# Counting keys for a top-64 search: one of VectorE's eight blocks handed to ScalarE

## The chip, the cores and the metric

The kernel runs on one core of a Trainium2 chip. The metric is device time in microseconds (us) of one execution. Three runs of the kernel before took 2841.61, 2842.69 and 2843.36 us, so the median is 2842.69 us.

The engines are called by their names in the profile: PE is TensorE (matrix products), PEld its weight loads, ACT is ScalarE, DVE is VectorE, POOL is GpSimd and SP is SyncE. Each works through its own instruction list in order and waits for others by semaphores.

## The reference, cut to what matters

Two transformer layers on eight sequences of 512 tokens. The part that the change touches is the attention of the first layer: 16 heads, 64 memory keys ahead of the sequence's own keys, a causal mask, and of each row's scores only the 64 largest kept.

```python
dots = jnp.einsum('bhid,bhjd->bhij', q, k) * SCALE
dots = jnp.einsum('bhij,hk->bkij', dots, pre_proj)
...
kth = jax.lax.top_k(dots, TOPK)[0][..., -1:]
dots = jnp.where(dots < kth, mask_value, dots)
attn = jax.nn.softmax(dots, axis=-1)
attn = jnp.einsum('bhij,hk->bkij', attn, post_proj)
out = jnp.einsum('bhij,bhjd->bhid', attn, v)
```

Beside it stand a feed-forward part quantised to 4 bits and, after it, a second layer. They aren't touched.

## The kernel before, in words

**Stages.** After some 150 us of preparation the attention of all eight sequences runs as one long planned stage, up to about 2287 us; the rest (the feed-forward part of seven sequences and the second layer) follows behind a branch on a flag and takes 552 us.

**Groups and blocks.** The attention is cut into 64 groups, eight for each sequence, in the order 7, 0, 5, 2, 6, 1, 4, 3 (`ORDER`). A group holds eight blocks. A block is a tile of 128 rows (16 heads by 8 tokens) by all the keys that these tokens can see: 72 keys for the first block of group 0, 8 more for each block on, 576 for the last block of group 7. Four groups are in flight at once, since the ring of score buffers has four places.

**The way of a group.** PE makes the scores and ACT copies them out of PSUM (L1037, L1043). The search (L1181) then looks for a threshold in each row that about 60 scores exceed. `begin` puts a first guess into `cur`. A round counts, block by block, how many scores lie above `cur` (`count`, L1072), and `narrow` (L1088) makes a better threshold from the eight counts. After the last round, `off` says how far the count is from the aim, `under` (L1135) takes the eight scores next to the threshold (two passes of DVE over each block), and `pick` (L1145) takes the one of them that is the 64th. ACT makes the exponentials (L1158), DVE keeps those that pass (L1167) and inverts their sum (L1252), POOL makes the mixing matrices `mixd` (L1260), and PE turns the scores with them (L1283) and multiplies with the values (L1307); ACT copies each product out of PSUM (L1289, L1321).

**The rounds.** Each round is a pair: how many of the eight blocks ACT counts, and whether POOL does `narrow` (else DVE does). In `ROUNDS`, the rule for 58 of the 64 groups, ACT counts all eight blocks of the first three rounds and POOL narrows; DVE counts all eight of the last three and narrows twice, and after the third it makes `off`. `EDGE`, for the first two groups, shares five rounds half and half between ACT and DVE. `LAST`, for the last four groups (60 to 63), has three rounds on ACT, two shared half and half, and a sixth on DVE alone.

**Two kinds of counts.** ACT's count is a Sign with a sum, so a block yields below minus above; DVE's is a comparison times -2, so it yields -2 times the number above. `base` holds, for each number of blocks on ACT, what has to be added to make both the same quantity; `narrow` begins with `base - raw` (L1099). The last round before was DVE's alone, and its `off` (L1209) is made with fixed numbers.

**What sets the order.** A planner written in Python (`Plan`, L81) orders every engine's list before the kernel runs. Each operation has an engine, an estimated cost, the operations that it needs and a due time; whichever is ready first on its engine goes next, the earlier due one where two are close. So a change of one operation's engine moves many others. DMAs of this stage are issued by SP, and none belongs to the search.

## Time and profile before

The profiled execution took 2840.84 us, of which the span from the first to the last instruction is 2839.1 us.

| | busy us | share of the span | instructions |
|---|---|---|---|
| PE | 2539.6 | 89% | 19064 |
| PEld | 1966.9 | 69% | 19064 |
| DVE | 2439.3 | 86% | 7978 |
| ACT | 2026.9 | 71% | 5876 |
| POOL | 1206.7 | 43% | 2215 |

| count of a block | instructions | busy us | mean ns |
|---|---|---|---|
| on ACT (L1079) | 1560 | 864.0 | 560 |
| on DVE (L1083) | 1512 | 828.0 | 580 |

The shares are means over the whole span, over stages with different limits. In the 40 slices of the profile PE is nine tenths busy or more from the second slice to the 30th, while DVE stands between eight and nine tenths and ACT between seven and eight. In the 31st and 32nd slice (about 2129 to 2271 us) PE falls to six tenths and less, and DVE stays at nine. That is why the prediction reads windows of time and not the page's totals alone.

### The profile page before, as it was taken

What the parts mean: (1) busy time and instruction counts of PE and PEld (TensorE: products, weight loads), DVE (VectorE), ACT (ScalarE), POOL (GpSimd) and SP (SyncE); (2) the same over time, 40 slices, a digit from 0 to 9 for tenths busy, and PEclk for the clock granted to TensorE, in tenths of its full rate; (3) what the DMA queues carried; (4) which work ended last, traced back from release to release, by engine and by line L of the source; (5) the groups of instructions that cost most, each with busy time, mean ns of one, the idle gap of its engine ahead of it and who ended that gap; (6) DMA issues with size and microseconds to landing.
All of it is one profiled execution on the core that took longest, in us unless ns stands there. A gap on an engine that the chain in (4) does not pass through costs nothing. (4 is left out here: it accounts for less than half of the span.)

```text
span 2839.1 us, 57481 instructions
## 1 busy us (share of the span) xinstructions
PE 2539.6 (89%) x19064; PEld 1966.9 (69%) x19064; DVE 2439.3 (86%) x7978; ACT 2026.9 (71%) x5876; POOL 1206.7 (43%) x2215
## 2 busy tenths in 40 slices
PE   5999999999999999999999999999986578999997
PEld 3677777777777778777787777778765455666664
DVE  6678989989989998999899889999999969877762
ACT  3478887788788878887888788788897444644442
POOL 3203544345444544444453545455445344444320
PEclk9999999999999999999999999999987788999998
DMA  4300010100000000000000010000110031000000
GB/s 135 148 24 16 27 30 16 29 18 19 21 25 18 28 18 27 20 18 26 21 19 18 25 29 17 16 23 20 35 42 5 8 109 30 23 16 15 8 8 15
DMA packets 114871, 82.70 MB, mean 29 GB/s; under 512 B 79339, under 2 KB 108806, under 8 KB 113798
## 3 DMA queue, kind: packets, MB, share of 16 engines
q1 hardware_dynamic: 114566, 78.95, 9.1%
q8 instruction: 153, 2.51, 0.4%
q14 instruction: 152, 1.25, 0.1%
HBM read 44.04 MB, written 35.39 MB: 28 GB/s over the span
## 5 line engine op out<-in xcount | busy, mean ns | idle before, releaser
L1079 ACT ACTIVATE junk<-ring,cur 128x312 int8<-128x312 f32 (+27 forms) x1560 | 864.0, 560 | 32.9 <-POOL cur L1132 12.0
L1083 DVE SCALAR_TENSOR_TENSOR junk<-ring,cur,two 128x72 int8<-128x72 f32 (+9 forms) x1512 | 828.0, 580 | 19.7 <-POOL cur L1132 17.7
L1037 PE MATMUL ps_sc<-xnT,tk 128*128 128x8 f32 (+38 forms) x2048 | 536.4, 408 | 37.3 <-ACT ring L1043 36.9
L997 PE MATMUL ps_mi<-rows,mg 128*128 128x128 f32 x4096 | 501.9, 277 | 10.5 <-ACT tk L1008 10.5
L997 PEld LDWEIGHTS ps_mi<-rows,mg 128*128 128x128 f32 x4096 | 480.5, 192 | 39.0 <-issue 13.8
L1037 PEld LDWEIGHTS ps_sc<-xnT,tk 128*128 128x128 f32 x2048 | 348.4, 199 | 185.8 <-issue 89.8
L1283 PE MATMUL ps_at<-mixd,ring 128*128 128x128 f32 (+1 forms) x3072 | 410.4, 284 | 63.1 <-POOL mixd L1260 58.5
L1283 PEld LDWEIGHTS ps_at<-mixd,ring 128*128 128x128 f32 (+1 forms) x3072 | 365.1, 185 | 96.0 <-POOL mixd L1260 72.4
L1167 DVE SCALAR_TENSOR_TENSOR ring<-ring,kth,e 128x520 f32<-128x520 f32 (+56 forms) x512 | 276.1, 561 | 86.2 <-ACT e L1158 84.1
L1099 POOL TENSOR_TENSOR cur<-base,raw 128x8 f32<-128x8 f32 x186 | 50.1, 269 | 658.7 <-ACT junk L1079 626.8
L1079 ACT ACTIVATION_READ_ACCUMULATOR junk<-ring,cur 128x1 f32 x1560 | 303.5, 195 | 0.0
L1289 ACT COPY at<-ps_at 128x512 f32<-128x512 f32 (+1 forms) x384 | 221.9, 581 | 101.5 <-PE ps_at L1283 98.3
L1140 DVE SCALAR_TENSOR_TENSOR y<-ring,cur 128x520 f32<-128x520 f32 (+56 forms) x512 | 288.7, 564 | 3.1
L1043 ACT COPY ring<-ps_sc 128x456 f32<-128x456 f32 (+56 forms) x512 | 184.4, 374 | 125.0 <-PE ps_sc L1037 120.4
L1143 DVE MAX8 top<-y 128x8 f32<-128x520 f32 (+56 forms) x512 | 255.3, 499 | 17.6
L1158 ACT ACTIVATE e<-ring 128x520 f32<-128x520 f32 (+56 forms) x512 | 228.2, 472 | 19.6 <-DVE ring L1167 19.4
L1307 PE MATMUL ps_y<-at,v 128*64 128x64 f32 (+1 forms) x6144 | 225.3, 225 | 16.9 <-ACT at L1289 16.8
L1307 PEld LDWEIGHTS ps_y<-at,v 128*64 128x64 f32 (+1 forms) x6144 | 198.7, 138 | 55.7 <-ACT at L1289 31.6
L1122 POOL TENSOR_TENSOR by<-gap,minus 128x8 f32<-128x8 f32 x124 | 220.5, 1779 | 9.7
L1008 ACT COPY tk<-ps_mi 128x256 f32<-128x256 f32 x512 | 168.0, 377 | 59.4 <-PE ps_mi L997 58.7
L1260 POOL TENSOR_TENSOR mixd<-mix,rden 128x512 f32<-128x512 f32 x128 | 153.1, 1212 | 132.8 <-DVE rden L1252 85.2
L235 PE MATMUL ps_gu<-mg,ring 128*128 128x352 f32 x448 | 148.8, 477 | 15.2 <-DVE hid L235 10.3
(316 smaller groups left out, 3934.7 us busy)
## 6 DMA issues: line engine op xcount, KB each, us to landing
msd<-scr SPq DMA_DIRECT2D x32, 512.0 KB
ring<-msd SPq DMA_DIRECT2D x512, 32.0 KB
scr<-in_L_attn_x_dram SPq DMA_DIRECT2D x10, 512.0 KB
mg_d<-mg SPq DMA_DIRECT2D x1, 4096.0 KB
att<-o SPq DMA_DIRECT2D x64, 64.0 KB
ring<-in_L_attn_x_dram SPq DMA_DIRECT2D x8, 512.0 KB
ring<-att SPq DMA_DIRECT2D x8, 512.0 KB
out_dram<-ring SPq DMA_DIRECT2D x8, 512.0 KB
```

The lines of the kernel that those rows point to most:

```text
L997: nc.tensor.matmul(ps[:, j * P : (j + 1) * P], mg[:, e, k + j, e2 * P : (e2 + 1) * P], toks(e), start=(e == 0), stop=(e == DC - 1),)
L1037: nc.tensor.matmul(ps[:, :ntok], q["tk"][side_of(g)][e][:, b].rearrange("p k i -> p (k i)"), o["xnT"][:, e, :ntok], start=(e == 0), stop=( ...
L1079: nc.scalar.activation(junk, src, AF.Sign, bias=thr, scale=-1.0, accum_out=raw[:, b : b + 1])
L1083: nc.vector.scalar_tensor_tensor(junk, src, thr, two.to_broadcast([P, src.shape[-1]]), ALU.is_ge, ALU.mult, accum_out=raw[:, b : b + 1],)
L1122: eng.tensor_tensor(by, gap[:, 1], minus, ALU.pow)
L1140: nc.vector.scalar_tensor_tensor(y, src, cur[:, 0, b : b + 1], src, ALU.is_ge, ALU.subtract, reverse1=True)
L1143: nc.vector.max(out=top[:, b, :], in_=y)
L1158: nc.scalar.activation(e, src, AF.Exp, scale=1.0 / SMALL)
L1167: nc.vector.scalar_tensor_tensor(src, src, kth[:, b : b + 1], e, ALU.is_ge, ALU.mult, accum_out=den[:, b : b + 1])
L1283: nc.tensor.matmul(pt[:n, b * P : (b + 1) * P], s[:, 4 * j + b, col : col + n], w["mix"][j][:, b, :], start=True, stop=True,)
L1289: nc.scalar.copy(ats[c][:n, :, j * 4 * RB : (j + 1) * 4 * RB].rearrange("p k (b i) -> p b k i", i=RB), w.pop(("pt", c, j))[:n].rearrange(" ...
L1307: nc.tensor.matmul(w["py"][j * DH : (j + 1) * DH, q * GR : (q + 1) * GR], vs[c][:n, k * DH : (k + 1) * DH], ats[c][:n, k, :], start=(c == ...
```

## The change

In `ROUNDS`, ACT now counts one block of eight, the first and so the shortest, in each of the three rounds that DVE had alone. In `LAST`, for the last four groups, the sixth round is shared half and half like the two before it. `EDGE` stays. As the last round may now hold counts of both kinds, `off` is made from `base` like the start of `narrow`; it comes out twice as large as before, with the sign kept, so the constants `io8` that it is compared with are doubled. `base` gets a fourth tile, for one block on ACT.

```diff
-ROUNDS = ((GB, True), (GB, True), (GB, True), (0, False), (0, False), (0, False))
+ROUNDS = ((GB, True),) * 3 + ((1, False),) * 3
 
 EDGE = ((GB // 2, False),) * (len(ROUNDS) - 1) + ((0, False),)
-LAST = ((GB, True),) * 3 + ((GB // 2, False),) * 2 + ((0, False),)
+LAST = ((GB, True),) * 3 + ((GB // 2, False),) * 3
...
             for q in range(8):
-                r.gpsimd.memset(io8[:, q : q + 1], 3.5 - q)
+                r.gpsimd.memset(io8[:, q : q + 1], 7.0 - 2 * q)
...
                         w["off"] = st.tile([P, GB], F32, name="foff", bufs=4)
-                        nc.vector.tensor_scalar(w["off"], w["raw"], -0.5, -AIM, ALU.mult, ALU.add)
+                        nc.vector.tensor_tensor(w["off"], base[na][:, g * GB : (g + 1) * GB], w["raw"], ALU.subtract)
```

In the instruction lists of the two kernels DVE's counts go from 1512 to 1322 and ACT's from 1560 to 1750. DVE instructions that take a round's counts (L1099, L1209) and name a wait for ACT go from 12 to 121, and ACT counts that name a wait for DVE from 12 to 124. The planner orders all engines anew.

## The prediction

> **What bounds the kernel now.** The chain of waits comes first and helps little: it only reaches back to 2287 us, where the last stage begins behind a branch, and the change lies before that. So I read the busy time in windows. I cut the attention stage where PE's slices fall: 150 to 2105 us, with full flow, and 2105 to 2266 us, where the last groups run out. Columns: busy of PE, PEld, DVE, ACT, POOL with instruction counts, granted clock, DMA.

> ```profile
> 150.00:2105.00 1955.00, 1829.97 (x15558) 1478.26 (x15556) 1782.69 (x6549) 1609.93 (x5026) 873.86 (x1821) 0.98 0.08 23
> 2105.00:2266.00 161.00, 97.43 (x748) 78.27 (x749) 154.59 (x467) 104.51 (x289) 69.30 (x105) 0.78 0.02 7
> ```

> In the full flow PE is busy 93.6%, DVE 91.2%, ACT 82.3%. In the run-out DVE is busy 96%, PE 61%, ACT 65%: there DVE alone sets the pace. Next I ask what PE waits for in the full flow, from the waits of PE in that window (waiting line, what it waited for, total us, times, longest).

> ```profile
> PE ps_at L1283 <- POOL mixd L1260: 41.9, 33, 3.4
> PE ps_sc L1037 <- ACT ring L1043: 32.6, 18, 4.1
> PE ps_y L1331 <- ACT y L1321: 19.2, 7, 2.8
> PE ps_mi L997 <- ACT tk L1008: 10.5, 7, 1.7
> PE ps_y L1307 <- ACT at L1289: 9.9, 8, 1.9
> PE ps_mi L968 <- ACT scr L974: 4.0, 1, 4.0
> ```

> All of PE's gaps together are some 120 us: 41.9 us because `mixd` is late, which is DVE's lateness passed on (POOL makes `mixd` once DVE has inverted the sums), and 76 us in these five ACT rows because a copy out of PSUM is late. PE's work doesn't change, so 120 us is all that the full flow could ever give, and the change takes load from the first kind of wait and adds it to the engine behind the second.

> Last, the four longest waits of ACT in the same window.

> ```profile
> ACT ring L1043 <- PE ps_sc L1037: 115.9, 158, 1.6
> ACT at L1289 <- PE ps_at L1283: 90.3, 111, 2.6
> ACT tk L1008 <- PE ps_mi L997: 51.8, 54, 1.6
> ACT scr L974 <- PE ps_mi L968: 21.8, 15, 2.4
> ```

> ACT's idle time, 345 us, is mostly waiting for PE: it has room, but it is held in order in front of PE's products.

> The row first: by busy time PE (93.6%) stands ahead of DVE. [...] I side with the row, because PE's list has only 120 us without work.

> **What is moved.** In 58 groups three counts of the first block go from DVE to ACT: 174. In the last four groups four counts each: 16. That is 1512 - 1322 = 190 in all.

> *DVE, saved.* The mean count of the eight sizes that a first block can have (72, 136, ... 520 keys) is 528, 361, 418, 485, 553, 792, 690, 750 ns. Two are swollen by operations on POOL beside them: at 72 and 392 keys, where the next block, 8 keys longer, takes 279 and 625 ns. With these two in their place the mean is 520 ns. Consecutive counts overlap by 70 ns (in the timeline one of 544 keys lasts 0.77 us and the next instruction starts after 0.69), so 0.45 us is freed each: 174 x 0.45 = 78 us, 87 us with the swollen means.

> *ACT, added.* 371, 411, 459, 507, 569, 628, 678, 741 ns, mean 545; in the timeline the next instruction follows 10 ns earlier, with the reading of the sum inside: 174 x 0.535 = 93 us.

> Both engines then stand at 87% in the full flow (1782.69 - 78 and 1609.93 + 93 over 1955). The trade is poor for small groups (72 keys: 371 ns on ACT for 279 on DVE) and even for large ones. [...]

> *Waits, added.* Each of the 174 counts waits for DVE's `cur`, and DVE's next step (L1099, or L1209 in the last round) waits for ACT's count. The trace has this in the first two and last four groups: 18 steps at L1099 with shared rounds, with DVE idle 3.9 us in 3 of them. So 0.22 us on average, 1.3 us where it happens. From below zero (15 of 18); from above 1.3 us each, 226 us. I take 0.22 for DVE, nearest in kind: 38 us. Behind a waiting L1099 or L1209 stand the passes of `under` and the keeping passes L1167, for which POOL's `mixd` and then PE wait. L1209 is placed straight after the counts, long before `pick` needs it, so its wait is avoidable but paid. Behind a waiting ACT count stand the copies out of PSUM, for which PE waits. The nearest row is ACT before its counts for POOL's `cur`: 11.5 + 10.6 + 4.0 us over some 175 rounds, 0.15 us each, 26 us for 174, and hidden unless PE needs the copy.

> *Small edits.* `off` stays one instruction of 8 numbers (L1209 170 ns, L1099 166 ns): nothing. `base` gets one tile more, 9 settings of 0.1 to 0.15 us on POOL, 1 us in the preparation, where POOL is busy 41 of 120 us; were it not covered, 1 us. No DMA is added, and no queue of SP or POOL is passed.

> **The sum, against the profiled execution (span 2839.1, time 2840.84 us).**

> - Full flow: DVE is relieved of 78 - 38 = 40 us net. PE sees that only through `mixd`'s 41.9 us. Bounds: nothing, and all of it. I take half, -21 us. ACT's work grows by 93/1610 = 6%, and 26 us of holds come on top, another 1.6%; PE's waits for it, 76 us, grow by 0 at best, and at worst by the whole 93. I take 15%, twice the growth in load, as a queue near full grows faster than its load: +12 us. Together -9 us.
> - Run-out: 16 counts at 0.36 to 0.71 us, less the overlap, are 7.4 us, and the last groups of the other kind finish there too, about 2 us. ACT has a third of its time free, so I take four new waits of 0.22 off: -8 us.

> 2840.84 - 17 = 2823.8 us; the median of the runs is 1.85 us above the profiled execution, so 2826 us. The ends: all of `mixd`'s wait and nothing from ACT give 2793 us; nothing from `mixd` and all 93 us on PE give 2928, which would need that ACT never counts while it waits for PE, though it waits 345 us: I don't reach so far. Three quarters of `mixd` with 5% give 2808, a quarter with 20% 2840; the new order of all lists, which no row prices, I put within these.

> **Rivals.**

> *PE holds the full flow, and the run-out gives only half.* For it: 93.6% busy. Against it: `mixd` is late 33 times. -4 us: 2839, within 0.2%.

> *DVE sets the pace.* For it: beside 91% busy it waits 108 us, 82 of them for exponentials (L1167 on L1158), so it has little air. Against it: those waits come from ACT, which gets fuller. The net 40 us pass in full, plus 8: 2795.

> *ACT is late (slower).* One mechanism: an ACT count that waits for `cur`, or comes between, holds a PSUM copy, and PE stops; and DVE stops at L1099 and L1209. The gains above are 21 + 8 = 29 us, so it decides from 29/174 = 0.17 us per handover that reach PE. At one wait in five of 1.3 us, 0.26 us, it costs 45 us: +16, 2859. For it: PE's longest waits (4.1, 4.0 us) are already on ACT. Against it: 15 of 18 such handovers were free, and ACT mostly waits for PE.

> *The change doesn't do what it says:* excluded, as the lists show the 190 counts moved.

> **Chances.** Forecast 0.45 (its own range 2808 to 2840), DVE paces 0.14, PE holds 0.16, ACT late 0.25. About 0.2% (5.7 us) is what a measurement here can tell from no change. Faster 0.59, same 0.16, slower 0.25. The range 2795 to 2862 takes in the middles of all four and leaves out the outer half of the two far ones.

> **What would show it.** DVE's busy time in the attention stage falls by 75 to 90 us and ACT's rises by 85 to 100. PE's wait for `mixd` falls to about half; its waits for ACT's copies grow to some 90 us. DVE shows new idle time at L1099 and L1209, 20 to 60 us. The run-out shortens by 5 to 10 us; the last stage stays at 552 us. I am wrong if PE's waits for ACT grow by more than 30 us, or if the full flow shortens by over 35.

## The result and the profile after

The changed kernel took 2857.59 us (median of 5 runs, 2855.38 to 2860.08) beside 2842.69 us for the kernel before (5 runs, 2841.61 to 2846.22). The ratio is 1.0051, with a 95% interval of 1.0038 to 1.0063. So the change made the kernel 15 us slower, where 17 us faster had been forecast. The profiled execution took 2857.65 us (span 2855.9).

First the two windows of the prediction, now of the kernel after (busy of PE, PEld, DVE, ACT, POOL, granted clock, DMA).

```profile
150.00:2105.00 1955.00, 1836.98 (x15446) 1474.03 (x15447) 1714.87 (x6161) 1674.87 (x5310) 854.78 (x1799) 0.98 0.08 23
2105.00:2266.00 161.00, 106.46 (x824) 83.95 (x821) 142.99 (x450) 125.48 (x377) 74.38 (x120) 0.82 0.03 7
```

DVE fell from 1782.69 to 1714.87 us and ACT rose from 1609.93 to 1674.87, as the change intends. PE is as full as before, 1836.98 of 1955 us. Over the whole attention stage, up to the point where the last stage begins (2287 us before, 2304 after) and with the preparation, DVE was relieved of 69 us (2041.33 to 1972.30) and ACT loaded with 91 us (1782.62 to 1873.71). The last stage itself took some 552 us, as before.

Next what PE waited for in the full flow, 150 to 2105 us, in the kernel after.

```profile
PE ps_sc L1037 <- ACT ring L1043: 63.4, 54, 4.6
PE ps_mi L997 <- ACT tk L1008: 16.9, 17, 2.6
PE ps_y L1307 <- ACT at L1289: 13.3, 20, 3.0
PE ps_at L1283 <- POOL mixd L1260: 7.5, 8, 1.6
PE ps_mi L926 <- ACT v L935: 4.9, 7, 1.1
```

The wait for `mixd` went from 41.9 to 7.5 us, more than forecast. But the copies out of PSUM took its place: `ring` went from 32.6 to 63.4, and all rows on ACT together from 78.6 to 108.8 us. PE's gaps sum up to nearly what they were: 120.5 us in all the rows before, 116.3 after.

ACT's own waits in that window show the other side.

```profile
ACT ring L1043 <- PE ps_sc L1037: 93.3, 133, 1.7
ACT at L1289 <- PE ps_at L1283: 57.7, 97, 1.7
ACT tk L1008 <- PE ps_mi L997: 38.3, 41, 1.7
ACT junk L1079 <- POOL cur L1132: 23.5, 27, 2.5
ACT junk L1079 <- DVE cur L1132: 14.4, 17, 1.2
```

It waits less for PE (115.9 to 93.3 at `ring`, 90.3 to 57.7 at `at`), since its added work falls into that time. The handovers are the last row and DVE's side of it: 14.4 us for ACT, and for DVE 4.9 us at L1099 (3.9 before) and 0.7 at L1209.

Where the time went that DVE was spared, its longest wait in that window says, first before, then after.

```profile
DVE ring L1167 <- ACT e L1158: 81.9, 67, 3.0
```

```profile
DVE ring L1167 <- ACT e L1158: 129.9, 97, 9.4
```

DVE had 68 us less to do in the window and waited 48 us longer for ACT's exponentials.

**Where the 15 us are.** I marked each group by the start of its reciprocal (L1252, one per group) and subtracted the marks of before.

| group | 2 | 10 | 18 | 26 | 34 | 42 | 48 | 50 | 55 | 57 | 59 | 61 | 63 |
|---|---|---|---|---|---|---|---|---|---|---|---|---|---|
| before, us | 288.0 | 543.6 | 799.5 | 1055.4 | 1311.4 | 1567.4 | 1768.9 | 1823.4 | 1977.9 | 2040.2 | 2106.8 | 2184.2 | 2265.6 |
| after, later by | 0.3 | 6.8 | 3.5 | 6.8 | 3.3 | 6.4 | -0.3 | 3.1 | 8.8 | 8.8 | 15.8 | 15.5 | 10.9 |

Two things are seen. Up to group 48 nothing was gained and nothing lost: the mean from group 2 to group 50 is 255.9 us per sequence before and 256.4 after. And from group 50 to group 59 the kernel after loses some 13 us. These are two questions, and the experiments take them apart. After the mark of group 63 another 6.3 us are lost (21.3 us to the start of the last stage before, 27.6 after), which no run takes apart: POOL makes the last `mixd` 2.4 us after the mark, behind two operations of the feed-forward part, where it took 0.4 before, and the last product (L1331) takes 5.41 us, where it took 3.72.

The largest single loss is at group 59. DVE's timeline in the kernel after there (start, length, instruction, idle time ahead of it and its releaser):

```profile
2098.67 0.43 DVE L1167 SCALAR_TENSOR_TENSOR ring<-ring,kth,e 128x208 f32<-128x208 f32 x1
...
2107.52 0.44 DVE L1167 SCALAR_TENSOR_TENSOR ring<-ring,kth,e 128x216 f32<-128x216 f32 x1 [8.41 <-ACT e L1158]
```

The same instruction in the kernel before:

```profile
2102.48 0.44 DVE L1167 SCALAR_TENSOR_TENSOR ring<-ring,kth,e 128x216 f32<-128x216 f32 x1 [2.93 <-ACT e L1158]
```

In the kernel after DVE stands still for 8.41 us because an exponential isn't there. ACT's list there says why: all eight counts of another group come first, and five more after them.

```profile
2098.66 0.68 ACT L1079 ACTIVATE junk<-ring,cur 128x456 int8<-128x456 f32 x1
...
2103.42 0.71 ACT L1079 ACTIVATE junk<-ring,cur 128x512 int8<-128x512 f32 x1
...
2106.68 0.43 ACT L1079 ACTIVATE junk<-ring,cur 128x168 int8<-128x168 f32 x1
...
2107.10 0.38 ACT L1158 ACTIVATE e<-ring 128x216 f32<-128x216 f32 x1
```

ACT isn't idle in these 8.4 us, and none of the 13 counts is one that the change added: they are ordinary counts in an order that the planner made anew.

### The profile page after: what moved, and what is told of

Its sections match the earlier page's. It is cut to its first block, busy times and chain, and to the rows that moved or that the text cites. A ratio compares the mean times of both kernels' runs of the same rounds, so it can differ in the third digit from the quotient of the medians.

```text
span 2855.9 us, 57796 instructions
## 1 busy us (share of the span) xinstructions
PE 2561.4 (90%) x19064; PEld 1972.2 (69%) x19064; DVE 2369.9 (83%) x7598; ACT 2118.1 (74%) x6256; POOL 1199.1 (42%) x2224
## 5 line engine op out<-in xcount | busy, mean ns | idle before, releaser
L1079 ACT ACTIVATE junk<-ring,cur 128x520 int8<-128x520 f32 (+43 forms) x1750 | 968.1, 559 | 66.3 <-POOL cur L1132 24.9
L1083 DVE SCALAR_TENSOR_TENSOR junk<-ring,cur,two 128x400 int8<-128x400 f32 (+12 forms) x1322 | 727.9, 587 | 11.4 <-POOL cur L1132 8.6
L1037 PE MATMUL ps_sc<-xnT,tk 128*128 128x8 f32 (+38 forms) x2048 | 550.2, 411 | 76.5 <-ACT ring L1043 76.0
L997 PE MATMUL ps_mi<-rows,mg 128*128 128x128 f32 x4096 | 513.7, 280 | 19.9 <-ACT tk L1008 16.9
L997 PEld LDWEIGHTS ps_mi<-rows,mg 128*128 128x128 f32 x4096 | 489.4, 195 | 49.1 <-ACT tk L1008 21.6
L1037 PEld LDWEIGHTS ps_sc<-xnT,tk 128*128 128x128 f32 x2048 | 346.5, 197 | 235.2 <-ACT ring L1043 100.0
L1283 PE MATMUL ps_at<-mixd,ring 128*128 128x128 f32 (+1 forms) x3072 | 407.6, 283 | 27.2 <-POOL mixd L1260 25.4
L1283 PEld LDWEIGHTS ps_at<-mixd,ring 128*128 128x128 f32 (+1 forms) x3072 | 370.1, 186 | 67.1 <-POOL mixd L1260 30.8
L1167 DVE SCALAR_TENSOR_TENSOR ring<-ring,kth,e 128x520 f32<-128x520 f32 (+56 forms) x512 | 278.3, 561 | 146.0 <-ACT e L1158 143.1
L1099 POOL TENSOR_TENSOR cur<-base,raw 128x8 f32<-128x8 f32 x186 | 57.8, 311 | 775.7 <-ACT junk L1079 697.1
L1079 ACT ACTIVATION_READ_ACCUMULATOR junk<-ring,cur 128x1 f32 x1750 | 342.0, 195 | 0.0
L1289 ACT COPY at<-ps_at 128x512 f32<-128x512 f32 (+1 forms) x384 | 221.7, 580 | 71.2 <-PE ps_at L1283 70.4
L1043 ACT COPY ring<-ps_sc 128x456 f32<-128x456 f32 (+56 forms) x512 | 186.3, 376 | 97.1 <-PE ps_sc L1037 95.9
L1307 PE MATMUL ps_y<-at,v 128*64 128x64 f32 (+1 forms) x6144 | 223.4, 225 | 22.0 <-ACT at L1289 21.6
L1307 PEld LDWEIGHTS ps_y<-at,v 128*64 128x64 f32 (+1 forms) x6144 | 196.8, 138 | 64.9 <-ACT at L1289 39.2
L1158 ACT ACTIVATE e<-ring 128x520 f32<-128x520 f32 (+56 forms) x512 | 230.7, 475 | 4.3 <-DVE ring L1167 3.8
L1008 ACT COPY tk<-ps_mi 128x256 f32<-128x256 f32 x512 | 173.1, 378 | 46.5 <-PE ps_mi L997 45.9
L1260 POOL TENSOR_TENSOR mixd<-mix,rden 128x512 f32<-128x512 f32 x128 | 150.2, 1192 | 68.9 <-DVE rden L1252 36.8
L235 PE MATMUL ps_gu<-mg,ring 128*128 128x352 f32 x448 | 149.1, 478 | 14.9 <-DVE hid L235 10.3
```

The lines of the kernel that those rows point to most:

```text
L235: call = lambda: fn(*a, **k)
L997: nc.tensor.matmul(ps[:, j * P : (j + 1) * P], mg[:, e, k + j, e2 * P : (e2 + 1) * P], toks(e), start=(e == 0), stop=(e == DC - 1),)
L1037: nc.tensor.matmul(ps[:, :ntok], q["tk"][side_of(g)][e][:, b].rearrange("p k i -> p (k i)"), o["xnT"][:, e, :ntok], start=(e == 0), stop=( ...
L1079: nc.scalar.activation(junk, src, AF.Sign, bias=thr, scale=-1.0, accum_out=raw[:, b : b + 1])
L1083: nc.vector.scalar_tensor_tensor(junk, src, thr, two.to_broadcast([P, src.shape[-1]]), ALU.is_ge, ALU.mult, accum_out=raw[:, b : b + 1],)
L1158: nc.scalar.activation(e, src, AF.Exp, scale=1.0 / SMALL)
```

## Experiments

All of them are the kernel before or the kernel after with the edit shown. A ratio is against the kernel before, run beside it on the same chip (its median lay between 2842.69 and 2844.33 us). "Pace" is the time from one group's mark to that of the same group of the next sequence. Where an edit adds a line, the line numbers of its rows are higher by one or two (L1038 is then L1037).

### The two halves of the change

**rounds_only** has the new `ROUNDS` and the old `LAST`, **last_only** the reverse.

```diff
-LAST = ((GB, True),) * 3 + ((GB // 2, False),) * 3
+LAST = ((GB, True),) * 3 + ((GB // 2, False),) * 2 + ((0, False),)
```

> Only the change of ROUNDS (174 counts of first blocks go to ACT); LAST as before. Theory 1 (the counts on ACT hold up the copies out of PSUM near the end of the attention stage, where the feed-forward part also needs ACT; the steady flow stays at 256 us for a sequence): about 2862 us, since LAST's gain of some 5 us in the run-out is missing. Theory 2 (LAST's shared sixth round is what costs): 2840 us or less.

> Only the change of LAST (16 counts in the last four groups go to ACT, the sixth round is shared); ROUNDS as before. Theory 1: 2834 to 2840 us, since DVE sets the pace of the run-out. Theory 2: 2855 us or more. The general form of off is in both and should cost nothing.

rounds_only: 2852.88 us, 1.0038 [1.0026, 1.0051]. Its marks stand where the kernel before has them up to group 48 (-2.8 us) and 9.6 us later at group 59: a loss of 12 us in between, with the same wait of 8.41 us. last_only: 2838.42 us, 0.9978 [0.9969, 0.9987]. Its pace in the flow is that of before, 256.0 us, and its mark of group 63 comes 8.7 us earlier (1.4 of them are there at group 48). Its last stage begins 5.6 us earlier. So the small half of the change is a gain by itself, and the loss comes with the other. The halves don't add up: +8.6 and -5.9 us on this chip, where both together are 14.9 us slower; the planner made another order for each.

### Order or load?

The planner makes new lists when a count changes engine. **list_kept** has the old lists with the counts done as in the kernel after, so that the loads are new and the order old:

```diff
-FAR = 32000.0
+PLANNED = {(1, 3): 0, (1, 4): 0, (1, 5): 0, (GB // 2, 5): 0}; FAR = 32000.0
...
-    pl.add("ACT", 0.28 + 0.00083 * n, one_count, deps + [tail]) if b < na else
+    pl.add("ACT", 0.28 + 0.00083 * n, one_count, deps + [tail]) if b < PLANNED.get((na, k), na) else
```

**list_only** is the reverse: the lists of the kernel after, and the moved counts done by DVE.

```diff
-    count(g, s, w["cur"], w["raw"], b, b < na)
+    count(g, s, w["cur"], w["raw"], b, b < DONE.get((na, k), na))
...
```

(`DONE` holds the same entries as `PLANNED`, and the steps behind the counts take their `base` by it.)

> The changed kernel's counts on ACT, but every engine's list in the order of the kernel before: the planner is told that DVE still does them, and each moved count stands in ACT's list where the plan had it for DVE. The lists of PE are the same as before to the last line. Theory 1 (load and waits of the moved counts cost the time): slower than before, 2852 to 2870 us, and not better than the changed kernel, because here ACT's list wasn't planned for them. Theory 3 (the new order of all lists costs the time, the moved counts by themselves gain): 2815 to 2838 us.

> The reverse: every engine's list in the order of the changed kernel, but the counts done by DVE as before, each in DVE's list where the plan had it for ACT. Theory 1: the order by itself costs little, ACT has its old load: 2838 to 2850 us, with DVE's lateness back in PE's waits. Theory 3: slower than before, 2855 us or more, as the order has no relief of DVE to pay for it.

list_kept: 2877.39 us, 1.0107 [1.0087, 1.0127]. list_only's total says nothing, since its own flag was set and the branch with the exact search ran (8280 us); everything up to the flag can be read. PE's waits in the full flow, first in list_kept, then in list_only:

```profile
PE ps_sc L1037 <- ACT ring L1043: 49.3, 45, 4.6
PE ps_at L1283 <- POOL mixd L1260: 33.6, 32, 2.4
```

```profile
PE ps_sc L1037 <- ACT ring L1043: 64.2, 42, 5.3
PE ps_mi L997 <- ACT tk L1008: 22.8, 17, 3.5
PE ps_mi L902 <- ACT v L938: 13.9, 1, 13.9
PE ps_y L1307 <- ACT at L1289: 11.5, 15, 1.6
```

Together with the two kernels this makes a square:

| | old lists | new lists |
|---|---|---|
| old loads | `mixd` 41.9, `ring` 32.6; pace 255.9 | `mixd` no row (under 1 us), `ring` 64.2; pace 256.4 |
| new loads | `mixd` 33.6, `ring` 49.3; pace 261.2 | `mixd` 7.5, `ring` 63.4; pace 256.4 |

This was the surprise of the study. With the new lists, PE doesn't wait for `mixd` even where DVE has all its old work, and it waits 64 us for `ring` even where ACT has none of the new. Both the wait that went and the wait that came belong to the order. The loads alone cost 5 us per sequence in the old order and nothing in the new one.

The same pair settles the end. From group 50 to group 59 the kernel before takes 283.4 us, the kernel after 296.1, list_only 299.6 and list_kept, whose whole pace is slower, 287.6. In list_only ACT has none of the moved counts, and still the same 13 counts stand ahead of the same exponential:

```profile
2112.52 0.44 DVE L1167 SCALAR_TENSOR_TENSOR ring<-ring,kth,e 128x216 f32<-128x216 f32 x1 [7.65 <-ACT e L1158]
```

### The loads one by one, in the old lists

**dve_short** takes from DVE and gives ACT nothing (in the last three rounds of the 58 groups the first block is read at 8 keys, and the flag is set to zero by hand); **act_extra** is the other way round. **dve_extra** is act_extra with `False`: the extra count on DVE.

```diff
-            src = block(s, g, b)
+            src = block(s, g, b)[:, :8] if short else block(s, g, b)
...
```

```diff
+                        if na == b == 0 and rounds is ROUNDS:
+                            count(g, s, w["cur"], st.tile([P, GB], F32, name="raw2", bufs=8), b, True)
```

> The kernel before with all its lists, but in the last three rounds of the 58 ordinary groups VectorE's count of the first block reads 8 keys instead of all of them (so these counts are wrong and the flag is set to zero by hand, so that the branch behind it isn't taken). ScalarE gets nothing. This is the relief of VectorE alone, some 50 to 60 us of its time. Theory 'ScalarE's copies': PE's wait for mixd falls from 42 to 10 us or so, nothing grows in its place, and the pace falls from 256.0 us per sequence to 252 or 253: 2815 to 2822 us in all. Theory 'clock grid' (the pace of the sequences has locked to the 3.413 us windows in which PE's clock is granted, 75 of them to a sequence): the pace stays at 256.0 us, with PE's waits appearing elsewhere, and the time is 2837 to 2844 us; or it goes down by a whole window to 252.6.

> The kernel before with all its counts, plus 174 counts of the first block on ScalarE at the places where VectorE counts it, into a sum that nobody reads. This is ScalarE's load alone, 93 us, with nothing taken from VectorE and VectorE waiting for none of it. Theory 'ScalarE's copies': PE's waits for copies out of PSUM grow and the pace goes to 260 us or so per sequence, 2870 to 2885 us in all (the counts on ScalarE in the old order took 261.5 us per sequence with VectorE relieved). Theory 'waits between the two engines': the load alone costs little, under 10 us, and what the counts in the old order cost (30 us) came from VectorE's waiting for ScalarE. Theory 'clock grid': either 256.0 us again, or a pace that isn't locked.

> The kernel before with each of the 174 counts of the first block done a second time on VectorE, into a sum that nobody reads: 78 us more on VectorE, nothing on ScalarE. If VectorE sets the pace, all of it shows, 10.8 us per sequence: 266.8 us, 2920 us. If it stands close behind PE, some of it does: 259.4 us, 2865 to 2875 us. If it has air, as its relief by 6.5 us per sequence without any gain suggests, 256.0 us stays in the flow, and only the last groups, where VectorE is busy 96%, pay some 3 to 6 us: 2846 to 2849 us. The old order on ScalarE, with the same counts there, cost 45 us.

dve_short: 2840.36 us, 0.9990 [0.9981, 0.9999]. act_extra: 2887.59 us, 1.0154 [1.0141, 1.0168]. dve_extra: 2854.46 us, 1.0036 [1.0023, 1.0048]. In two sequences (1025 to 1537 us) dve_short relieves DVE of 13.1 us (468.73 to 455.65), and PE's waits there are these:

```profile
PE ps_at L1283 <- POOL mixd L1260: 10.5, 10, 2.4
PE ps_sc L1037 <- ACT ring L1043: 10.3, 4, 4.1
```

Before, they were 11.8 and 8.9. So DVE's relief isn't passed on: DVE only waits longer for the exponentials (22.1 to 34.2 us in that stretch), which come when ACT's list comes to them. Its load does count upwards, but not in full: 78 us more cost 10.8. ACT's load in the old order costs 45 us for 89 us of work (1871.21 beside 1782.62 us up to the last stage), with no handover back to DVE, and PE's waits show the place: `ring` 46.0 instead of 32.6 us in a window that holds less of the flow, as the marks run 262 us apart.

### What the pace is made of

To see whether the pace is locked to the grid, I changed PE's work by a little, once per sequence. **pe_extra** does the scores of one block twice (the cut shown), **pe_three** three times (`3` in place of `2`), **pe_half** only half of the repeat (one more product ahead of the loop):

```diff
-                    for e in range(DC):
+                    for e in list(range(DC)) * (2 if g == ORDER[2] and b == 3 else 1):
```

> The kernel before with four matmuls of 264 or so keys done twice, once in each sequence (the scores of the fourth block of one group): 1.0 us of PE's time more per sequence, 8 us in all, with no list changed. If PE's work simply sets the pace, it goes from 256.0 to 257.0 us per sequence and the time to 2850 or 2851 us. Theory 'clock grid': the pace stays at 256.00 us to a tenth of a us, the us goes out of the waits or out of the half-rate windows, and the time stays within 2 us of the kernel before's.

> As with the score matmuls of one block per sequence done twice, but only half of that work: two more records of 352 keys, about 0.7 us of PE's time per sequence (the whole repeat is four records of some 0.35 us, 1.4 us per sequence, not 1.0 as its text said), 5.7 us in all. Theory 'clock grid': the pace is a whole number of 3.413 us windows, so 256.0 us per sequence (75) or 259.4 (76), and not between; the time is that of the kernel before, within 2 us, or that of the whole repeat, 2861 to 2866 us. Theory 'PE's work, with a factor' (1.4 us of work cost 2.6 us): half of it, 257.3 us per sequence, 2853 us.

> The same block's score matmuls done three times: eight more records of 352 keys, 2.8 us of PE's time per sequence, 23 us in all. Theory 'clock grid': 259.4 us per sequence again (76 windows), so 2862 to 2867 us, or 262.8 (77 windows), 2888 to 2894 us. Theory 'PE's work, with a factor': 261.2 us per sequence, 2884 us. If PE's work passed one for one: 258.8 us per sequence, 2866 us; the first two can be told apart by the marks of the sequences in the trace, not by the time alone.

The block has 352 of the sequence's own keys, and the repeat cost 1.2 us per sequence (PE's rows of that shape went from 10.8 to 20.2 us in eight sequences). **pe_less_1** and **pe_less_4** make the scores of one or four blocks from half of the features, **short_less_4** adds dve_short to the latter; the flag is set to zero by hand in all three.

```diff
-                    for e in range(DC):
+                    few = 1 if g == ORDER[2] and 3 <= b < 7 else DC
+                    for e in range(few):
...
```

> The kernel before, but the scores of one block per sequence (the fourth of group 5) are made from the first half of the features only, so PE has two records of 352 keys less, about 0.65 us per sequence; these scores are wrong, and the flag is set to zero by hand. Theory 'clock grid': 256.0 us per sequence again, so 2840 to 2845 us, or a whole window less, 252.6 us and 2814 to 2820 us. Theory 'PE's work passes smoothly': 255.3 us, 2838 us.

> The same for four blocks per sequence (the fourth to the seventh of group 5): eight records less, about 2.6 us of PE's time per sequence. Theory 'clock grid' with PE's work behind it: 252.6 us per sequence (74 windows), 2814 to 2820 us. If VectorE or ScalarE holds the pace at 256.0 us, nothing moves: 2840 to 2845 us.

> Both reliefs: PE's four half blocks as before, and VectorE's first block read at 8 keys in the last three rounds of the 58 ordinary groups (so both the scores and the counts are wrong, and the flag is set to zero by hand). If VectorE stood close behind PE, its relief counts once PE has less to do: a window or more below what PE's relief alone gives, so 249.2 us per sequence and 2785 to 2795 us where the other gives 252.6. If VectorE has no say, the same pace as with PE's relief alone, within 3 us in all.

| kernel | PE's work per sequence, us | last paces, us | windows | time, us | ratio |
|---|---|---|---|---|---|
| before | | 255.97, 255.99, 255.99 | 75 | 2842.69 | |
| pe_half | +0.6 | 259.45, 259.44, 259.44 | 76 | 2859.99 | 1.0061 [1.0048, 1.0074] |
| pe_extra | +1.2 | 259.33, 259.79, 259.29 | 76 | 2863.68 | 1.0070 [1.0056, 1.0083] |
| pe_three | +2.4 | 262.83, 262.83, 262.82 | 77 | 2882.74 | 1.0113 [1.0088, 1.0138] |
| pe_less_1 | -0.5 | 255.87, 255.93, 255.99 | 75 | 2842.09 | 0.9987 [0.9978, 0.9996] |
| pe_less_4 | -1.8 | 255.99, 255.96, 256.01 | 75 | 2840.48 | 0.9984 [0.9974, 0.9995] |
| dve_short | | 256.96, 255.05, 256.91 | 150 for two | 2840.36 | 0.9990 [0.9981, 0.9999] |
| short_less_4 | -1.8 (not read apart) | 255.06, 256.88, 255.08 | 150 for two | 2836.22 | 0.9966 [0.9954, 0.9978] |
| dve_extra | | 257.14, 258.25, 257.18 | 151 for two | 2854.46 | 1.0036 [1.0023, 1.0048] |
| after | | 252.45, 259.12, 252.71 | 150 for two | 2857.59 | 1.0051 [1.0038, 1.0063] |

(pe_less_4's 1.8 us is half the difference of PE's busy time in 1025 to 1537 us, 479.63 and 475.95; pe_less_1's is a quarter of it, pe_half's and pe_three's half and twice that of pe_extra.) The pace of each of these kernels comes within 0.5 us of a whole number of windows for one sequence or for two. Not every kernel's does: act_extra's sequences take 260.9 to 265.1 us, and rounds_only, with the rounds of the kernel after in this stretch, takes 514.1 and then 512.5 us for two. 0.6 us of work cost 3.4 us per sequence, and twice as much next to nothing on top. My expectation for pe_extra, 256.00 again, was wrong, the step was there all the same. Two of pe_three's six runs took 2863.5 and 2866.3 us and four 2882.3 to 2884.3, which fits 76 and 77 windows, though only one run's trace was read. In these three kernels PE waits no more than before: its idle time stays at 16.2 us per sequence (group 10 to 42), while its time at half clock grows from 6.8 to 13.5 us in pe_half, 11.3 in pe_extra and 17.1 in pe_three. So the step is PE's own work, done longer at half clock.

Downwards there was no step: with 1.8 us less work on PE and 6.5 us less on DVE the pace stayed at 256.0, in each alone and in both together (256.0 us as the mean of two in short_less_4, which took 7.5 us less all the same: in its profiled execution the mark of group 2 is already 3.4 us early). PE's waits in pe_less_4 (1025 to 1537 us) say where the work that was taken away went.

```profile
PE ps_sc L1038 <- ACT ring L1044: 12.6, 4, 4.1
PE ps_at L1284 <- POOL mixd L1261: 11.8, 10, 2.4
```

`ring` has grown from 8.9 to 12.6, that is by the 3.7 us that PE was spared. So PE's own work didn't hold the pace from below, and DVE's didn't either; ACT's copies came when they came.

### The place

In six of the eight sequences of the kernel before, PE's longest wait stands ahead of the fifth score of group 1: the two buffers for scores hold the third and fourth, which ACT hasn't copied. PE's timeline, then ACT's, kernel before:

```profile
1047.92 1.98 PE L997 MATMUL ps_mi<-rows,mg 128*128 128x128 f32 x16
1053.97 2.27 PE L1037 MATMUL ps_sc<-xnT,tk 128*128 128x104 f32 x9 [4.08 <-ACT ring L1043]
```

```profile
1045.10 0.55 ACT L1043 COPY ring<-ps_sc 128x72 f32<-128x72 f32 x2
1045.55 0.68 ACT L1079 ACTIVATE junk<-ring,cur 128x456 int8<-128x456 f32 x1
...
1053.00 0.71 ACT L1079 ACTIVATE junk<-ring,cur 128x512 int8<-128x512 f32 x1
...
1053.71 0.21 ACT L1043 COPY ring<-ps_sc 128x88 f32<-128x88 f32 x1
```

Between the copies of the first two scores and that of the third, ACT's list has eight counts and six exponentials, 8.2 us. PE stops for 4.1 us, and its clock is halved (0.50) from 1053.05 to 1059.88 us, as the stop ends; so it is in all six of these sequences. **copy_spot_8** pulls the due times of these copies forward, in the kernel with the new last round alone. **late_old** is the kernel after with the old rounds in groups 48 to 59, and **late_spot** is both together.

```diff
-... LAST if n > len(groups) - 5 else ROUNDS)
+... LAST if n > len(groups) - 5 else ROUNDS if n < 48 else OLD)
```

```diff
+            fresh = pl.ops[pl.mark :]
             due(n, 0.5, 1.0)
+            for op in fresh:
+                if op.eng == "ACT" and g == ORDER[5]:
+                    op.due -= 8.0
```

> The changed kernel, but with the old rounds (VectorE alone in the last three) for groups 48 to 59; groups 2 to 47 and the last four have the change. Theory 'order at the end': the changed kernel loses its 15 us in groups 50 to 63, where ScalarE has up to 13 counts in a row ahead of the exponentials that VectorE waits for (8.4 us in one place); so the marks of group 59 come back to within 3 us of the kernel before, and the time is 2836 to 2844 us. Theory 'ScalarE is too full everywhere': groups 2 to 47 cost their share, and the time stays at 2850 us or more.

> The kernel with the new last round for the last four groups alone, in which the planner's due times of ScalarE's score copies of group 1 (one group per sequence) are 8 us earlier, so that they come between the counts and not behind eight of them. Theory 'ScalarE's list at that place holds the pace': PE's wait of 4.1 us there goes, the half-rate windows behind it too, and the pace falls by a window at least, to 252.6 us per sequence: 2812 to 2820 us. If the pace is held by many places at once, it stays at 256.0 us and the time at 2836 to 2842 us.

> The same earlier due times for the copies of group 1, in the kernel with the new rounds for groups 2 to 47, the old ones for 48 to 59 and the new last round. If VectorE's load counts once the place is mended: another window less than with the old rounds, 249.2 us per sequence, 2790 to 2800 us. If it doesn't: the same as with the old rounds, within 4 us; and if the added counts on ScalarE make new places of the kind: 5 to 20 us more than with the old rounds.

All four kernels of this square have the new last round:

| | lists as planned | copies of group 1 pulled forward |
|---|---|---|
| old rounds | 2838.42 us, 0.9978 [0.9969, 0.9987] | 2838.84 us, 0.9982 [0.9973, 0.9991] |
| new rounds in groups 2 to 47 | 2840.94 us, 0.9991 [0.9982, 1.0000] | 2809.55 us, 0.9882 [0.9867, 0.9898] |

late_old answers the question of the end: with the old rounds in groups 48 to 59 the mark of group 59 is back (2107.3, before 2106.8), and the time is 16.7 us below the kernel after's 2857.59, while groups 2 to 47 keep the change. The loss sat in the last groups.

Of the square's other entries, neither edit alone gives more than the new last round does by itself: 4.8 us with the earlier copies and 1.9 with the new rounds, beside its 5.9. Both together take the pace to 252.5 us on average (534.2 to 1796.8 us in five sequences) and the kernel to 2809.55 us, 34 us below the kernel before on the same chip (2843.66) and 48 below the kernel after, the fastest of this study. PE's waits in the full flow, first copy_spot_8, then late_spot:

```profile
PE ps_at L1283 <- POOL mixd L1260: 30.6, 18, 3.5
PE ps_sc L1037 <- ACT ring L1043: 28.9, 37, 2.2
...
PE ps_mi L968 <- POOL same L1109: 16.3, 5, 3.3
PE ps_mi L968 <- POOL cur L1099: 4.7, 2, 3.3
```

```profile
PE ps_sc L1038 <- ACT ring L1044: 51.3, 54, 4.1
PE ps_y L1308 <- ACT at L1290: 16.1, 26, 2.1
PE ps_at L1284 <- POOL mixd L1261: 9.4, 8, 3.5
```

In copy_spot_8 the long `ring` wait is gone (longest 2.2), but `mixd` still holds PE for 30.6 us and POOL's queue for another 21: in every sequence PE now stops for 3.25 us ahead of L968, a few us behind the mended place, and the stretch at half clock, 6.83 us, is still there. In late_spot `mixd` is 9.4, and no row for POOL's queue at L969 is left among the nine largest.

Why both edits together pay isn't shown. Each edit makes the planner order everything anew, so the square doesn't separate DVE's lighter load from the order that comes with it; dve_short together with the mended place would have, and it wasn't run. Nor did the second edit mend this place in the kernel with the new rounds, for it was gone there: in late_old, from 290 to 1800 us, no wait of PE over 1.5 us stands ahead of the fifth score of group 1. Its longest, 4.6 us, stands ahead of the third score of group 5. In late_spot that one is gone too, the longest in this stretch is 2.4 us, and per sequence (group 10 to 42) PE is idle 11.7 us beside 14.6 in late_old and at half clock 6.8 us beside 10.2. Whether another shift of due times would have done the same wasn't tried.

### More of the last round

**last_six** and **last_eight** are last_only with `LAST` for six and eight groups (`- 7` and `- 9` in place of `- 5`).

> The new last round for the last groups alone, with the old rounds before it, and the rule for the last groups taken for six groups instead of four (58 to 63). Half of VectorE's counts of three rounds of groups 58 and 59 go to ScalarE, 12 counts each, some 5 to 8 us of VectorE's time in a stretch where it is busy 91 to 96%. Theory 'VectorE sets the end': another 3 to 5 us come off, 2833 to 2836 us (four groups: 2838). Theory 'order': ScalarE's counts come in front of the exponentials of groups 57 to 59, as with the new rounds there, and the time is 2840 to 2850 us.

> The same with eight groups (56 to 63, the whole last sequence). Theory 'VectorE sets the end': 2830 to 2836 us. Theory 'order' and 'ScalarE is full': groups 56 and 57 stand in the full flow beside the last projections, ScalarE is late there, and the time is over 2845 us.

last_six: 2846.04 us, 1.0010 [1.0001, 1.0018]. last_eight: 2849.69 us, 1.0022 [1.0013, 1.0031]. last_six loses nothing up to group 59 (283.5 us from group 50, as last_only) but takes 159.5 us from there to group 63, where last_only takes 151.4; last_eight takes 287.7 and 158.2 us. From group 50 to 59 DVE waits 6.7 us in last_six and 18.8 in last_eight for ACT's counts at L1099 and L1209, and not at all in last_only. Of the three numbers of groups tried, only four pays.

## Why the prediction was wrong, step by step

Two steps failed. In the full flow it was the cause given for `mixd`'s wait, from which the gain of 21 us was taken. The sign of the result came from the new order of the lists, which the sum left without a price: between group 48 and group 59 the kernel after lost 16 us and list_only, with none of the added counts on ACT, 20; with the old rounds in groups 48 to 59 the loss was gone (late_old, 16.7 us less).

- **"41.9 us because `mixd` is late, which is DVE's lateness passed on."** This is the step that failed in the full flow. The row was read rightly, its cause was not looked for. DVE with 6.5 us less to do per sequence leaves `mixd` at 38.5 us in the full flow (dve_short); DVE with all its work and the new lists leaves none (list_only). `mixd` was late because of where things stood in the lists: DVE itself waited 82 us for exponentials, a row that I had quoted under a rival and set aside there.
- **"I take 15%, twice the growth in load", +12 us for PE's waits for ACT.** They grew by 30.2 us (78.6 to 108.8), the limit that I had named for being wrong. The size was off, and so was the reason: list_only has the same `ring` wait, 64.2, without any added load.
- **Full flow, "Together -9 us".** 0 up to group 48. PE's time without work in the window was 125.0 us before and 118.0 after, so a gain in one kind of wait became another kind; and the busy time of the same work isn't fixed, as the prediction took it to be: per sequence (group 10 to 42) PE was busy 239.8 us before and 241.1 after, with 6.8 and 7.7 us at half clock. The pace came out within 0.5 us of 150 windows for two sequences.
- **Run-out, -8 us.** Nearly right for the part that it spoke of: in last_only it is 7.3 us at the mark of group 63 and 6 us in the time (2838.42 beside 2844.33 for the kernel before on the same chip). In the kernel after the marks of group 59 and 63 come 4.9 us closer, covered by the 13 us that groups 50 to 59 lose ahead of them and the 6.3 us behind.
- **"The new order of all lists, which no row prices, I put within these."** That order made the loss, but for the 6.3 us behind group 63, which no run explains: in the flow it made and unmade the waits, at the end it put 13 counts before an exponential, as list_only shows without any added load. What could have been read ahead of time is ACT's new list, for long runs of counts between two copies or ahead of an exponential.
- **"0.22 us on average" for 174 handovers, 38 us on DVE.** Far too dear: 1.7 us more idle time at L1099 and L1209 together in the full flow, 0.01 us each. The likely reason is that DVE does the other seven counts meanwhile, so ACT's one is done. The row that I took the price from is of rounds shared half and half.
- **DVE saved 78 to 87 us, ACT added 93.** 69 and 91 by the busy times of the stage, for all 190 counts. ACT's was priced well; DVE's saving stayed under the 75 to 90 us that were named as a sign. Neither made the result.
- **The rival "ACT is late", 2859 us.** It gave the time nearly (+16 for +14.9) by another mechanism: it counted on handovers at 0.26 us each. So its nearness is chance. That an ACT count which comes between holds a copy and PE stops is true in the old order (act_extra, +45 us); at the end it holds an exponential, and DVE stops.
- **"I side with the row, because PE's list has only 120 us without work."** DVE wasn't the engine to relieve: dve_short's 0.9990 speaks against that, and by dve_extra a seventh of what DVE was given more showed (10.8 of 78 us). But the row named no better engine: 1.8 us less work for PE per sequence gave 0.9984 (pe_less_4).

## What to carry to other kernels

Before pricing an engine's relief, follow the wait one step further than the engine that it names: ask what the late engine itself waits for, since a busy engine may be late because of the order of a third one's list. Where a planner orders the work, look at the new lists for long runs of one kind ahead of a short thing that another engine needs; this takes no run, and here it was most of the loss. And when two edits give nothing each, try them together before dropping them: here they gave 34 us, though the runs don't show why.

## What the runs showed of the hardware

The pace of this kernel's attention, with PE busy 93.6% of the full flow, settled on whole numbers of the 3.413 us steps in the record of the granted clock, 75, 76, 77 for a sequence or 150, 151 for two, within 0.5 us in all ten kernels of the table. So 0.6 us of extra PE work cost 3.4 us per sequence (pe_half, 259.44), the next 0.6 us nothing (pe_extra), and 1.8 us less work gained nothing (pe_less_4). The step upwards was work done longer at half clock (6.8 us per sequence before, 13.5 in pe_half), not waiting (16.2 us idle in both). The paces of before close in on 256.00 as 255.56, 255.88, 255.95, 255.97, 255.99; why they do wasn't shown. Not every kernel's pace is such a whole number: late_spot's sequences take 249.6 to 253.5 us, act_extra's 260.9 to 265.1.
